# Where the first layer's Gelus stand beside a selective scan, and how its feature pipeline is paced

## The chip, the cores and the metric

The kernel runs on one core of one Trainium2 chip. The metric is the device time of one execution in microseconds; the median of three executions before the change is 9565.78 us (9564.62 to 9581.03). Five engines take part: TensorE (PE) for matmuls, VectorE (DVE), ScalarE (ACT), GpSimd (POOL) and SyncE (SP), whose queue issues the DMAs. Each engine works through its own instructions in order, and engines wait for one another by semaphores.

## The reference, cut to what matters

Four layers run one after another on an input of 4 images, 128 channels, 64x64 pixels. The change lies in layer 0, which is computed per image as follows (the names are those of the reference):

```python
feat = _gelu(_dwconv2d(x_adapted, conv1_w, conv1_b))           # first depthwise 3x3 convolution
ca = feat.mean((2, 3))
ca = sigmoid(maximum(ca @ ca1_w.T, 0.0) @ ca2_w.T)             # attention of channels
feat = _gelu(_dwconv2d(feat * ca[:, :, None, None], conv2_w, conv2_b))
scores = sigmoid(einsum('bchw,oc->bohw', feat, head_w)[:, 0] + head_b[0])
pv = jnp.var(x_adapted, axis=1, ddof=1)
final_scores = 0.7 * scores + 0.3 * sigmoid(pv * 10.0)
sm = final_scores.reshape(B, Hp, PS, Wp, PS).mean((2, 4)).reshape(B, Hp * Wp)
idx = jnp.argsort(-sm, axis=1)                                 # 256 patches of 4x4 pixels, sorted
...
x1n = layernorm(reordered x + pe[order])
...
dA = jnp.exp(dt[..., None] * A)
dBx = dt[..., None] * Bc[:, :, None, :] * xc[..., None]
def step(h, inp):                                              # selective scan over 4096 positions
    dA_t, dBx_t, C_t = inp
    h = dA_t * h + dBx_t
    return (h, jnp.einsum('bds,bs->bd', h, C_t))
...
out = (y * silu(z)) @ out_proj_w.T, put back in the old order
```

Before it stands a group norm of x (`_gn`). Layer 1 is a 3x3 convolution, layers 2 and 3 hold attention and expert layers; together they take the larger part of the time.

## The kernel before, in words

Layer 0 is the function `layers01`. For each of the four images (b = 0 to 3) there are two kinds of work.

The first kind is the generator `in_order(b, ...)`. It loads the image, computes the group norm (`K.groupnorm_scale`, L178), writes the normed image with a margin of one pixel (`xp`, by `K.groupnorm_fill`, L230 on ACT, eight chunks of 512 pixels), runs the first depthwise convolution with its Gelu (`first`), the attention of channels, the second convolution with its Gelu (`second`), the scores (`gauged`, with a Tanh), the sort of the patches (`sort`), the layer norm over positions (`ask`, `placed`, `centred`, `varied`, `scaled_by_root`), and at last the permutation (`turn`, `sorted_`), whose result `xq` is the sequence that the scan reads. The convolutions read their input in rows with 32 channels and three shifts laid over the partitions; so the padded image is stored to DRAM (`stored`, L458) and gathered again as `under` (`gather`, L467), three DMAs a chunk, all in SP's queue.

The second kind is `scan`. It goes through 32 chunks (4 images times 8 chunks of 512 positions). A chunk has eight groups g of two states each, and a group has two slots (i = 0 and 1), so that a chunk has 16 slots. A group begins on DVE with one multiplication (`hs`, L915) that reads `b_ps` from PSUM, where PE has spread the factors B (`spread_b`). Each slot then has two exponentials on ACT (`decay`, L922), two scans on DVE (L926), a copy of the last state (`carry`, L929) and a multiplication by C (L930) on POOL, and PE sums over states (`y_ps`, four matmuls in each odd slot, for the group before). There are two buffers for `decay` and one for `b_ps`.

The order of the scan stage is written out by hand: `tc.manual_schedule` keeps the order in which instructions are issued for all five engines. The order comes from turns. While the scan of image b runs, `in_order(b + 1)` is advanced by one turn in each slot, up to slot 110; what is left then is run at once in slot 111 (`until`, seven of eight chunks), since the entry of the next image's first chunk, in the eighth, reads `xq`. Two further things come beside the scans in each chunk: the entry of the next chunk (`enter`, with a Silu in slot 3, an Exp and a Ln in slot 7, POOL's work and eight DMAs `dt` and `dtx` in slots 8 to 11) and the gate (`gate`, issued in slot 8, its Silu in slot 9).

Matmuls are issued in the turn itself. What ACT, DVE or POOL does with their results is put off by `later` to the next `K.flush`, which comes in the next slot after that slot's two exponentials and before its scans. So a Gelu whose convolution is issued in an odd slot runs on ACT in the even slot that follows, behind that slot's exponentials. PE's part of a slot is issued in this order: `add` for the group before (odd slots), entry, turn, and in even slots `spread_b` at the end.

`staged(n, period, *stages)` is a software pipeline: every `period` turns another of n chunks starts, and each active chunk is advanced by one stage a turn. For both convolutions the stages are gather, nothing, nothing, convolution, nothing, next; `even()` waits for an even slot before each starts. `K.bank` gives out three PSUM banks in turn and flushes early where the oldest is still wanted. For b = 3 the scans have other work beside them (the end of images 2, 0 and 1), which is not touched.

For b = 0, `in_order` runs before the scans with nothing beside it, outside the hand-written order.

`Common` (L30 to L88) builds constants on DVE and POOL in one pool that stays for the whole kernel.

Of the kernel before, what the change touches and what calls it, by code (L numbers as in the profile page):

```python
# [30 lines left out]
class Common:  # L31
# [3 lines left out]
    def __init__(self, tc, pool):  # L35
# [33 lines left out]
        self.same4 = self.same_block("same4", 2)  # L69
        self.same16 = self.same_block("same16", 4)  # L70
        self.group_mean = pool.tile([P, P], F32, name="group_mean")
        nc.vector.tensor_scalar(self.group_mean, self.same4, 0.25, None, ALU.mult)

    def shifted(self, name, src, n, ops):

        nc = self.nc
        ti = self.pool.tile([P, n], I32, name=name + "_i")
        nc.vector.tensor_scalar(ti, src, *ops)
        tf = self.pool.tile([P, n], F32, name=name)
        nc.vector.tensor_copy(tf, ti)  # L80
        return tf

    def same_block(self, name, shift):
        nc = self.nc
        r = self.shifted(name + "_r", self.row_i, 1, (shift, None, ALU.arith_shift_right))
        c = self.shifted(name + "_c", self.col_i[:, 0:P], P, (shift, None, ALU.arith_shift_right))
        t = self.pool.tile([P, P], F32, name=name)
        nc.vector.tensor_scalar(t, c, r, None, ALU.is_equal)  # L88
        return t
# [194 lines left out]
def layers01(K, xd, dpool, w, w1):  # L284
# [8 lines left out]
    TURNS_END = 53  # L293
    ctx = ExitStack()
# [145 lines left out]
    def in_order(b, made, work, psum):  # L440
# [79 lines left out]
        yield from staged(NCH, 2, lambda c: gather(0, c), None, None, first, None, first_stored)  # L520
# [31 lines left out]

        def gauged(c):
# [5 lines left out]
            def tanh():  # L559
# [18 lines left out]
        for _ in range(2):  # L578
            next(tail)
            yield  # L580
# [3 lines left out]
        def sort():  # L584
            yield from wait(6)
# [49 lines left out]
        def centred(c):  # L635
# [42 lines left out]
        def scaled_by_root(n):  # L678
# [5 lines left out]
            def taken():  # L684
                rs = work.tile([P, CH], F32, name="ln_rs", tag="rs", bufs=1)
# [16 lines left out]
        yield from together(tail, sort(), staged(NCH, 2, ask, None, placed, centred, None, varied), backs())  # L702
# [1505 lines left out]
```

## Time and profile before

| | us |
|---|---|
| median of three executions | 9565.78 |
| the profiled execution | 9578.96 |
| its span, first to last instruction | 9577.2 |
| stage 1: `in_order(0)`, before the scans | 0 to 232 |
| stage 2: scans of images 0 to 2, `in_order(1 to 3)` beside them | 232 to 1976 |
| stage 3: scan of image 3, ends of images beside it | 1976 to 2638 |
| the rest: layers 1 to 3 | 2638 to 9577 |

The stages are told apart by the first multiplication L915 (232.4 us), by that of chunk 24 (1976.1 us) and by the last scan (2637.7 us). In the profile a line number is that of the kernel before. L92 is the matmul helper, and L144 is the line of `later`: instructions put off by it have its line, so they are told apart by the names of their tiles (`fp` is the first Gelu's output, `f` the second's, `sz` the gate's). A group of instructions is given with its number, busy time, mean duration of one, idle time of its engine before them and what ended that. "A <- B" in a list of waits means that A's engine stood idle and B's end released it.

### The profile page before, as it was taken

To read this page: it belongs to the slowest core of one execution; us is meant where nothing else is said; L and a number is where in the kernel's file an instruction comes from. 1 tells how busy PE (TensorE), PEld (TensorE's weight loads), DVE (VectorE), ACT (ScalarE), POOL (GpSimd) and SP (SyncE) were. 2 spreads that over 40 slices of the span, in tenths; PEclk is the share of its full clock that TensorE was granted. 3 is DMA by queue.
4 is the path that set the end of the run, shared out by engine and by line. 5 is a ranking of instruction groups with operands and counts; after the bars stand their busy time and mean duration, and the time that the engine had idled before them with its cause. 6 is when DMAs were issued, how large, how long until landed. Compare 5 with 4: busy or idle time off the path is not lost.

```text
span 9577.2 us, 189161 instructions
## 1 busy us (share of the span) xinstructions
PE 8608.8 (90%) x74394; PEld 3287.8 (34%) x74394; DVE 7159.3 (75%) x7845; ACT 7287.0 (76%) x10505; POOL 4933.0 (52%) x3287
## 2 busy tenths in 40 slices
PE   5887888889879999979999979999989999998787
PEld 2221222234443333333333333333333333334444
DVE  1889798987858888868888867888876888874464
ACT  3776767654449999969999969999978999984232
POOL 1677676765525555555555545555555555543011
PEclk8887888889989999989999989999989999999998
DMA  4434425222232221141222233221222222231205
GB/s 118 122 77 109 108 72 128 74 67 80 71 86 39 39 41 40 32 112 40 40 40 40 39 94 55 38 41 39 39 81 62 40 40 40 40 97 58 81 10 168
DMA packets 580323, 631.22 MB, mean 66 GB/s; under 512 B 118816, under 2 KB 374888, under 8 KB 578536
## 3 DMA queue, kind: packets, MB, share of 16 engines
q1 hardware_dynamic: 579432, 619.12, 27.5%
q8 instruction: 586, 9.60, 0.4%
q14 instruction: 305, 2.50, 0.1%
HBM read 444.74 MB, written 106.97 MB: 58 GB/s over the span
## 4 chain that ended last, share of the span: by engine, by line
PE 60%; DVE 4%; DMA 2%; POOL 2%; issue 2%; ACT 2%; SPq 0%; DVEq 0%; POOLq 0%; ACTq 0%
PE ctx_ps L92 27%; PE acc_ps L92 14%; PE score L92 12%; PE ln_xc L92 1%; DMA w<-in_L_ffn_weight 1%; PE hid_ps L92 1%; PE kv L92 1%; POOL ln_sd L1845 1%; PE ln_var L129 1%; DVE ctx L1498 0%; DMA queries<-head_d 0%; POOL q L1293 0%; PE pool L92 0%; DVE x L1998 0%; ACT hid L1685 0%
## 5 line engine op out<-in xcount | busy, mean ns | idle before, releaser
L1564 ACT ACTIVATE ex<-score 128x1024 f32<-128x1024 f32 x5120 | 4924.1, 1038 | 235.8 <-PE score L92 147.9
L92 PE MATMUL ctx_ps<-ex,qt 128*32 128x512 f32 x20480 | 2733.2, 606 | 19.7 <-DVE ctx L1498 19.7
L1513 POOL TENSOR_TENSOR folded<-ex 128x1024 f32<-128x1024 f32 x512 | 1223.3, 2389 | 2100.3 <-ACT ex L1564 1826.9
L1570 DVE STREAM_TRANSPOSE turned<-ex 128x1024 f32<-128x1024 f32 x1536 | 1885.3, 1227 | 337.1 <-ACT ex L1564 336.8
L1546 DVE STREAM_TRANSPOSE turned<-ex 128x1024 f32<-128x1024 f32 x1532 | 1841.9, 1202 | 0.0
L92 PE MATMUL acc_ps<-turned,turned_v 128*32 128x256 f32 x24576 | 1769.3, 379 | 3.0 <-POOL qt L1251 2.3
L926 DVE TENSOR_TENSOR_SCAN hs<-decay,carry,hs 128x512 f32<-128x512 f32 x1024 | 1245.4, 1265 | 196.9 <-ACT decay L922 183.8
L92 PE MATMUL score<-queries,keys 32*128 32x512 f32 x10240 | 1334.3, 497 | 51.9 <-POOL queries L1241 47.0
L92 PEld LDWEIGHTS acc_ps<-turned,turned_v 128*32 128x32 f32 x24576 | 800.8, 110 | 1476.6 <-issue 1324.4
L930 POOL TENSOR_TENSOR hs<-hs,c_sb 128x1024 f32<-128x1024 f32 x512 | 1207.0, 2357 | 70.4 <-DMA c_sb<-c_d 31.4
L922 ACT ACTIVATE decay<-dt,a_neg 128x512 f32<-128x512 f32 x1024 | 693.0, 689 | 659.8 <-DVE hs L926 649.8
L92 PEld LDWEIGHTS score<-queries,keys 32*128 32x128 f32 x10240 | 512.4, 182 | 1145.7 <-ACT ex L1564 777.7
L1370 POOL TENSOR_TENSOR turned_v<-v,quarter 128x1024 f32<-128x1024 f32 x256 | 612.9, 2395 | 264.8 <-PE acc_ps L92 222.5
L92 PE MATMUL y_ps<-hs,pair 128*64 128x512 f32 x2048 | 656.1, 769 | 32.2 <-POOL hs L930 32.2
L1514 POOL TENSOR_TENSOR quarters<-folded 128x512 f32<-128x512 f32 x512 | 657.6, 1284 | 40.1
L92 PEld LDWEIGHTS ctx_ps<-ex,qt 128*32 128x32 f32 x20480 | 406.4, 108 | 655.2 <-issue 599.1
L915 DVE TENSOR_TENSOR hs<-dtx,b_ps 128x2048 f32<-128x2048 f32 x256 | 579.8, 2265 | 54.9 <-PE b_ps L92 31.0
L92 PE MATMUL b_ps<-dbc,state 32*64 32x512 f32 x1024 | 340.8, 747 | 237.4 <-DVE hs L915 237.3
L929 POOL COPY carry<-hs 128x2 f32<-128x2 f32 x512 | 97.9, 191 | 688.3 <-DVE hs L926 659.6
L1564 ACT ACTIVATION_READ_ACCUMULATOR ex<-score 128x1 f32 x2048 | 439.0, 214 | 0.0
L1498 DVE COPY ctx<-ctx_ps 128x512 f32<-128x512 f32 x256 | 176.8, 691 | 329.3 <-PE ctx_ps L92 317.8
L1555 DVE TENSOR_REDUCE dacc<-quarters 128x2 f32<-128x512 f32 x508 | 326.9, 643 | 0.0
(376 smaller groups left out, 8785.0 us busy)
## 6 DMA issues: line engine op xcount, KB each, us to landing
c_sb<-c_d SPq DMA_DIRECT2D x512, 128.0 KB
keys<-head_d SPq DMA_DIRECT2D x1024, 64.0 KB
queries<-head_d SPq DMA_DIRECT2D x1024, 64.0 KB
under<-image_d SPq DMA_DIRECT2D x192, 264.0 KB
dt<-dt SPq DMA_DIRECT2D x128, 256.0 KB
dtx<-dtx SPq DMA_DIRECT2D x128, 256.0 KB
v<-value_d SPq DMA_DIRECT2D x1024, 32.0 KB
w<-in_L_ffn_weight SPq DMA_DIRECT2D x32, 1024.0 KB
```

The lines of the kernel that those rows point to most:

```text
L92: self.nc.tensor.matmul(out, lhsT, rhs, start=start, stop=stop)
L915: nc.vector.tensor_tensor(hs, dtx2, bb.unsqueeze(1).to_broadcast([P, NQ, CH]), ALU.mult)
L922: nc.scalar.activation(ex, dt2[:, q, :], AF.Exp, scale=a_neg[:, q, g : g + 1])
L926: nc.vector.tensor_tensor_scan(hs[:, q, :], decays[q - 2 * i], hs[:, q, :], carry[:, g, q : q + 1], ALU.mult, ALU.add)
L930: nc.gpsimd.tensor_tensor(hs[:, two, :], hs[:, two, :], cs.unsqueeze(1).to_broadcast([P, 2, CH]), ALU.mult)
L1370: nc.gpsimd.tensor_tensor(t, v.unsqueeze(2).to_broadcast([P, 4 * BT, 4, HD]), quarter.unsqueeze(1).to_broadcast([P, 4 * BT, 4, HD]), ALU.mult,
L1513: nc.gpsimd.tensor_tensor(hs, exs[:, :, 0], exs[:, :, 1], ALU.add)
L1514: nc.gpsimd.tensor_tensor(qs, hs[:, :, 0 : CH // 2], hs[:, :, CH // 2 :], ALU.add)
L1546: nc.vector.transpose(*upright)
L1555: nc.vector.tensor_reduce(at, qs, AX.X, ALU.add)
L1564: nc.scalar.activation(ex, sps[p], AF.Exp, scale=scale, accum_out=sums[:, t : t + 1] if summed else None)
L1570: nc.vector.transpose(*upright)
```

## The change

- In `staged` a new argument `quiet` names a stage. While any active chunk is about to run that stage, the whole pipeline is held until the slot within the chunk is one of 0, 8, 10, 12, 14 (`QUIET`). It is used for both convolutions of images 1 to 3 (stage 3 is the convolution; its Gelu follows in the next slot). For b = 0 it is off.
- The square for the patch variance (`pv_mean`, `pv_sq`) leaves `second` and becomes a stage of its own, `gauge`, one turn before the second convolution; `gauged` comes one turn later than before.
- For images 1 to 3 the padded image is filled two chunks in a turn.
- `sort` starts when all eight gauges are counted, instead of after a fixed number of turns; the two extra turns before it are gone.
- The position pipeline starts a chunk every 1.5 turns for images 1 to 3, instead of every 2.
- Tiles tagged `ln_sq` and `rs` get two buffers instead of one. To make room, the temporary tiles of `Common` move to a pool that is closed after use.

```diff
@@ -58,33 +58,35 @@
 
         self.row_i = pool.tile([P, 1], I32, name="row_i")
         nc.gpsimd.iota(self.row_i, pattern=[[0, 1]], base=0, channel_multiplier=1)
-        self.col_i = pool.tile([P, 256], I32, name="col_i")
-        nc.gpsimd.iota(self.col_i, pattern=[[1, 256]], base=0, channel_multiplier=0)
         self.col = pool.tile([P, 256], F32, name="col")
-        nc.vector.tensor_copy(self.col, self.col_i)
         self.row = pool.tile([P, 2], F32, name="row")
         nc.vector.tensor_copy(self.row[:, 0:1], self.row_i)
         nc.vector.tensor_scalar(self.row[:, 1:2], self.row[:, 0:1], 128.0, None, ALU.add)
 
-        self.same4 = self.same_block("same4", 2)
-        self.same16 = self.same_block("same16", 4)
-        self.group_mean = pool.tile([P, P], F32, name="group_mean")
-        nc.vector.tensor_scalar(self.group_mean, self.same4, 0.25, None, ALU.mult)
-
-    def shifted(self, name, src, n, ops):
+        with tc.tile_pool(reuse_waits="tile", name="temporary", bufs=1) as tmp:
+            self.col_i = tmp.tile([P, 256], I32, name="col_i")
+            nc.gpsimd.iota(self.col_i, pattern=[[1, 256]], base=0, channel_multiplier=0)
+            nc.vector.tensor_copy(self.col, self.col_i)
+            self.same4 = self.same_block("same4", 2, tmp, tmp)
+            self.same16 = self.same_block("same16", 4, tmp, pool)
...
@@ -291,6 +293,7 @@
 
     SLOTS = 2 * NG
     TURNS_END = 53
+    QUIET = (0, 8, 10, 12, 14)
     ctx = ExitStack()
     pool = lambda name, bufs, **kw: ctx.enter_context(tc.tile_pool(reuse_waits="tile", name=name, bufs=bufs, **kw))
     cst = pool("l0_const", 1)
@@ -402,11 +405,13 @@
             nc.sync.dma_start(out=t[:, at], in_=src[:, at])
         return t
 
-    def staged(n, period, *stages):
+    def staged(n, period, *stages, quiet=None):
 
 
         active, begun, turn = [], 0, 0
         while begun < n or active:
+            while any(a[1] == quiet for a in active) and K.slot % SLOTS not in QUIET:
+                yield
             if begun < n and turn >= begun * period:
                 active.append([begun, 0])
                 begun += 1
@@ -503,7 +508,9 @@
             fill(c)
             if c in (3, 5, 7):
                 stored(xp, 0, c // 2 - 1)
-            yield
+            if c % 2 or b == 0:
+                yield
+        quiet = 3 if b else None
         fp = kept["fp"] = big.tile([P, HW + 2, HW + 2], F32, name="fp", tag="mid")
         nc.gpsimd.memset(fp[:, 0, :], 0.0)
         nc.gpsimd.memset(fp[:, HW + 1, :], 0.0)
@@ -517,7 +524,7 @@
                 stored(fp, 1, c // 2)
 
         yield from even()
-        yield from staged(NCH, 2, lambda c: gather(0, c), None, None, first, None, first_stored)
+        yield from staged(NCH, 2, lambda c: gather(0, c), None, None, first, None, first_stored, quiet=quiet)
 
         def attention_of_channels():
             favg = small.tile([P, 1], F32, name="favg")
@@ -537,17 +544,16 @@
 
         begun = [0]
 
-        def gather_second(c):
-            gather(1, c)
-            begun[0] += 1
-
-        def second(c):
+        def gauge(c):
             mp = K.bank(psum, [P, CH], "pv_mean")
             mm(rect(mp), K.center, xp[:, 1 + 8 * c : 9 + 8 * c, 1 : HW + 1])
-            sq = squares[c] = work.tile([P, CH], F32, name="pv_sq", tag="ln_sq", bufs=1)
+            sq = squares[c] = work.tile([P, CH], F32, name="pv_sq", tag="ln_sq", bufs=2)
             later(nc.scalar.activation, sq, mp, AF.Square)
+
+        def second(c):
+            begun[0] += 1
             ps = convolved(unders.pop(c), deep2)
-            f2 = features[c] = work.tile([P, CH], F32, name="f2", tag="rs", bufs=1)
+            f2 = features[c] = work.tile([P, CH], F32, name="f2", tag="rs", bufs=2)
             later(nc.scalar.activation, f2, ps, AF.Gelu, bias=conv2_b, scale=ca)
 
         def gauged(c):
@@ -565,24 +571,29 @@
                     AX.XY,
                     ALU.add,
                 )
+                later(counted)
+
+            def counted():
+                gauges[0] += 1
 
             later(tanh)
 
-        seconds = staged(NCH, 2, gather_second, None, None, second, None, gauged)
+        gauges = [0]
+        seconds = staged(
+            NCH, 2, lambda c: gather(1, c), None, gauge, second, None, None, gauged, quiet=quiet
+        )
         channels = attention_of_channels()
         yield from even()
         tail = together(channels, seconds)
         while begun[0] < NCH:
             next(tail)
             yield
-        for _ in range(2):
-            next(tail)
-            yield
 
         perm = []
 
         def sort():
-            yield from wait(6)
+            while gauges[0] < NCH:
+                yield
             sp = K.bank(psum, [P, 256], "sm_ps")
             mm(sp, share.to_broadcast([P, P]), sm)
             later(nc.vector.tensor_copy, sm, sp)
@@ -639,7 +650,7 @@
             def taken():
                 if c == 0:
                     kept["xn"] = big.tile([P, 16, 256], F32, name="xn", tag="mid")
-                sq = squares[c] = work.tile([P, CH], F32, name="pos_sq", tag="ln_sq", bufs=1)
+                sq = squares[c] = work.tile([P, CH], F32, name="pos_sq", tag="ln_sq", bufs=2)
                 nc.scalar.activation(sq, mp, AF.Square)
                 for a in range(2):
                     nc.scalar.copy(inner(c, a), outer(mp, a))
@@ -682,7 +693,7 @@
                 nc.tensor.transpose(by_block[:, k], spreads[:, n, k : k + 1].to_broadcast([P, P]), K.ident)
 
             def taken():
-                rs = work.tile([P, CH], F32, name="ln_rs", tag="rs", bufs=1)
+                rs = work.tile([P, CH], F32, name="ln_rs", tag="rs", bufs=2)
                 nc.scalar.copy(rs, bp)
                 later(scaled, rs)
 
@@ -699,7 +710,7 @@
                 scaled_by_root(n)
                 yield from wait(2 if n < 4 else 1)
 
-        yield from together(tail, sort(), staged(NCH, 2, ask, None, placed, centred, None, varied), backs())
+        yield from together(tail, sort(), staged(NCH, 1.5 if b else 2, ask, None, placed, centred, None, varied), backs())
         yield
 
 
```

More of the change, by code (lines that the diff above doesn't have):

```diff
@@ L67, in __init__, with shifted, same_block @@
         nc.vector.tensor_scalar(self.row[:, 1:2], self.row[:, 0:1], 128.0, None, ALU.add)
-        self.same4 = self.same_block("same4", 2)
-        self.same16 = self.same_block("same16", 4)
-        self.group_mean = pool.tile([P, P], F32, name="group_mean")
-        nc.vector.tensor_scalar(self.group_mean, self.same4, 0.25, None, ALU.mult)
-    def shifted(self, name, src, n, ops):
+        with tc.tile_pool(reuse_waits="tile", name="temporary", bufs=1) as tmp:
[4 more added lines that the diff above has]
+            self.same16 = self.same_block("same16", 4, tmp, pool)
+            self.group_mean = pool.tile([P, P], F32, name="group_mean")
+            nc.vector.tensor_scalar(self.group_mean, self.same4, 0.25, None, ALU.mult)
+    def shifted(self, name, src, n, ops, pool=None):
         nc = self.nc
-        ti = self.pool.tile([P, n], I32, name=name + "_i")
+        pool = pool or self.pool
+        ti = pool.tile([P, n], I32, name=name + "_i")
         nc.vector.tensor_scalar(ti, src, *ops)
-        tf = self.pool.tile([P, n], F32, name=name)
+        tf = pool.tile([P, n], F32, name=name)
         nc.vector.tensor_copy(tf, ti)
         return tf
-    def same_block(self, name, shift):
+    def same_block(self, name, shift, tmp, pool):
         nc = self.nc
-        r = self.shifted(name + "_r", self.row_i, 1, (shift, None, ALU.arith_shift_right))
-        c = self.shifted(name + "_c", self.col_i[:, 0:P], P, (shift, None, ALU.arith_shift_right))
-        t = self.pool.tile([P, P], F32, name=name)
+        r = self.shifted(name + "_r", self.row_i, 1, (shift, None, ALU.arith_shift_right), tmp)
+        c = self.shifted(name + "_c", self.col_i[:, 0:P], P, (shift, None, ALU.arith_shift_right), tmp)
+        t = pool.tile([P, P], F32, name=name)
         nc.vector.tensor_scalar(t, c, r, None, ALU.is_equal)
```

## The prediction

> **What bounds the kernel now.** I began with the stages, because the change touches only the first two.
>
> ```profile
> core 0: us, PE busy (x) PEld busy (x) DVE busy (x) ACT busy (x) POOL busy (x), PEclk, DMA share, GB/s
> 0.00:232.00 232.00, 130.39 (x682) 50.41 (x682) 37.29 (x106) 77.48 (x115) 31.91 (x44) 0.89 0.45 111
> 232.00:1976.00 1744.00, 1428.29 (x5022) 420.85 (x5022) 1530.08 (x1230) 1194.80 (x1594) 1258.28 (x960) 0.83 0.39 98
> ```
>
> From 232 to 1976 us DVE is busy 1530 of 1744 us, more than any other engine. Its work there is fixed; what can be won is its idle time of 214 us. The waits of that stretch, and of three chunks of the first scan, say where it lies:
>
> ```profile
> DVE hs L926 <- ACT decay L922: 165.1, 97, 5.5
> ...
> DVE hs L926 <- ACT decay L922: 43.3, 21, 5.5
> ...
> DVE hs L926 <- ACT decay L922: 2.3, 3, 0.9
> ```
>
> The first line is the whole stage: 165 us of scans waiting for their exponentials. The second is chunks 1 to 3 of the first scan, where both convolutions run beside it; the same chunks of the next two show 44.1 and 42.5. The third is chunk 7, which has an entry and a gate but nothing else. So 130 of the 165 us come with the convolutions. The timeline of ACT and of DVE shows one such wait (slot 30):
>
> ```profile
> 355.31 1.28 ACT L144 ACT_TABLE_LOAD   x1
> 361.94 0.69 ACT L144 ACTIVATE fp<-conv,conv_b 128x512 f32<-128x512 f32 x1 [5.35 <-PE conv L92]
> 362.53 0.19 ACT L144 ACTIVATION_READ_ACCUMULATOR fp<-conv,conv_b 128x1 f32 x1
> 362.74 1.28 ACT L922 ACT_TABLE_LOAD   x1
> 364.03 1.30 ACT L922 ACTIVATE decay<-dt,a_neg 128x512 f32<-128x512 f32 x2
> ...
> 364.76 2.46 DVE L926 TENSOR_TENSOR_SCAN hs<-decay,carry,hs 128x512 f32<-128x512 f32 x2 [5.45 <-ACT decay L922]
> ```
>
> The Gelu sits between two table loads of 1.28 us, waits 5.35 us for its convolution, and the next exponentials stand behind it. The convolution was issued in the odd slot just before, and PE reached it late.
>
> **What each Gelu costs, before.** From the starts of the scans, with DVE's own work taken off, each slot's idle time follows. For the first eight Gelus (slots 28 to 42) it is 1.73, 5.41, 2.08, 0, 2.20, 3.97, 1.36 and 2.20 us, for the second eight with their Tanh (slots 48 to 62) 21.7 us together.
>
> **What one costs in an odd slot.** Behind an odd slot's scans (2.5 us) DVE has the multiplication L915 (2.26 us). How much of ACT's work this hides, other rows tell: the entry's Silus in slot 3 (1.28 + 0.69 + 0.68 + 1.28 = 3.93 us) leave 0.69 us of idle DVE; with a fill of 0.82 us in the same slot (4.75 us) 1.39 us. So about 3.3 us are free, and what exceeds them costs nearly all of itself. A Gelu with its two loads is 3.4 us (3.3 for `f`): 0.1 us.
>
> Here a rule speaks against the change. The Trainium skill ("ScalarE: Activation LUTs", What ACT_TABLE_LOAD costs) prices a switch of tables at 1283 ns and a drain of 1380 ns, 2.66 us in all. A Gelu would then take 6.2 us and cost 2.9 in each odd slot, and a gate slot with three switches 6.8; 36 and 12 of them make 186 us, more than the 130 lost now, so the kernel would come out some 75 us slower. The rows show the load alone: the exponential starts at 364.03, 1.29 us after its load began. I take 1.28.
>
> **The change, part by part**, for each of images 1 to 3:
>
> 1. *Gelus moved.* The order of the changed program puts the 16 Gelus in slots 25, 27, 29, 31, 33, 41, 43, 45 and 57, 59, 61, 63, 65, 73, 75, 77. Twelve are alone with their loads: 12 x 0.1 = 1.2 us. Four (25, 41, 57, 73) follow the gate's Silus in slot 9: 1.28 + 1.2 + 1.28 + 0.9 + 1.28 = 5.8 us, 2.4 us of DVE idle each, 9.6 in all. Entries in chunks 1 to 4 still wait some 1.2 us each, 5 us. The loads fall by only 12 in the whole program (446 to 434); they are not where the gain lies.
> 2. *Convolutions in even slots, PE.* The convolution (2.78 us) now stands ahead of `b_ps`, which the next L915 needs. In the trace PE stood idle 6.28 us before the `b_ps` at 340.22, waiting for L915 to release the bank, and that `b_ps` was done 3.3 us before it was needed: 6.28 - 2.78 + 3.3 = 6.8 us of slack. The Gelu no longer finds its convolution late. In turns of the second convolution PE's work for a group is 2.78 + 1.13 + 1.07 + 1.07 + 1.94 = 8.0 us against DVE's 4.80 + 2.26 + 0.66 = 7.7: seven groups, 2 us. If PE is cold (`b_ps` 1.97 us instead of 1.07), up to 7.
> 3. *SP's queue.* Gathers keep their three DMAs and three turns of lead; the first now stand ahead of the entry's `dt` and `dtx`, which wait for POOL. Behind a late gather stand the `c_sb` loads. Hidden, by the slack of part 2.
> 4. *Square apart, two buffers.* Square and Tanh (0.6 + 0.76 us) fall in even slots, under their 3.3 us: nothing; beside a Gelu they would cost 1.3 each.
> 5. *Fills in pairs.* 1.6 us of ACT in slots 14 to 17, under the same cover: nothing. It takes one fill out of slot 19, -0.7, which I leave in the rounding.
> 6. *What moves later.* Position work and sort go from chunks 4 and 5 (87.1 and 69.7 us in the trace) to 5 and 6, with eight positions in 12 slots instead of 16; the last `xq` falls in slot 111, a slot in which the rest runs in a burst. The instructions are the same, closer together, and POOL has 1.2 us more a position in the tight slots beside 2 x 2.55 a group. I take 4 us, and 1.5 for the burst (a permutation: transposes, copy, matmul, copy, about 5 us in the first stage, half of it hidden). Bounds -2 and +15.
>
> The second rule weighed bears on part 6. In the sort an operation of DVE that reads two SBUF tiles has these rows, beside the scans and in the first stage:
>
> ```profile
> L598 DVE SCALAR_TENSOR_TENSOR eq<-sm,cl,before x6: 2393/2412/2431, 561.8 to 1734.7; 128x256 f32<-128x256 f32 x6
> ...
> 143.85 0.48 DVE L598 SCALAR_TENSOR_TENSOR eq<-sm,cl,before 128x256 f32<-128x256 f32 x1
> ```
>
> 2.41 us instead of 0.48. The skill ("SBUF — State Buffer", SBUF: two separate sides) says why: such an operation and one of POOL take a shared pair of ports in turn, for a whole instruction. By the rule, with POOL fuller, all ten such operations of a sort could be held by some 2 us, 20 us in place of some 9 now (12.9 us in the trace's chunk 4, 3.9 by the shortest rows): +11 an image. By the rows most are held already, by the C multiplications that stay. I take 0 and keep +11 within the +15.
>
> Sum for an image: before 43.3 + 2.4 (chunk 4) = 45.7; after 1.2 + 9.6 + 5 + 2 = 17.8; gain 27.9, less 5.5 for part 6: 22.4. For three: 67.
>
> 7. *Stage 1.* Two things of it change the path:
>
> ```profile
> 19.62 2.39 SPq L402 DMA_DIRECT2D xb<-in_x  x4
> ...
> 46.84 8.72 PE L92 MATMUL conv<-under,deep 96*32 96x512 f32 x48 [13.82 <-DMA under<-image_d]
> ...
> 164.39 0.58 ACT L686 COPY ln_rs<-pos_rs 128x512 f32<-128x512 f32 x1 [1.76 <-POOL xn L691]
> ```
>
> With the temporary pool the weights' loads wait for DVE's constants, and the changed order puts the image ahead of them. The image lands by some 11 us (it took 9.8 in the trace), the constants by 13, the norm and fill by 24; the weights, 19 us of issuing, by 32. The stores of `xp` stand behind them: 32 instead of 35.3, without the fill's pace (4.5 us for four); convolutions near 41.5: -5.3, between 0 and -10. The second `rs` buffer frees ACT and POOL from one another in the five last scalings: 2.35 us becomes POOL's 1.7, -3.3. Together -8.
>
> Total -75. The profiled execution, 9578.96 us, would become 9504; it stands 13.2 us above the median, so for the median 9565.78 - 75 = 9491 us.
>
> **Rivals.** *A, as summed*: 9460 to 9520 alone. *B, the delayed position work gives much back*: part 6 costs 18 us an image instead of 5.5, as its full +15 and PE half cold would make it; (27.9 - 18) x 3 + 8 = 38, 9528 us. For it: chunk 4 already has PE waiting for POOL (41.5 us over the three scans, longest 6.8). Against: POOL is busy 62.8 of 87.1 us there. *C, a convolution holds up `b_ps`, slower*: if a gather lands late, PE stops in an even slot with `b_ps` behind, and L915 waits, DVE with it. The trace has convolutions waiting for `under` 17.4 us in 7 cases, 3.3 at most in the one before slot 30. It decides from the slack of 6.8 us: 75/48 = 1.6 us beyond it at each of 48 convolutions undo the gain, 2.8 us make it 9625. *D, no real change*: the holds only move the idle time, as ACT's 165 us partly turn into waits for PE; within 19 us of the time before.
>
> **How the numbers follow.** A 0.66, B 0.18, C 0.09, D 0.07. I call 0.2% (19 us) what a measurement can tell: A and B are faster (0.84), D the same (0.07), C slower (0.09). The range takes in A, B and the bounds of parts 6 and 7: from 9455 (part 6 at -2 in each image, -22; stage 1 at -13, -5; Gelus behind the gate at 1.7 us, -8) to 9545 (B, with nothing won in stage 1, and 9 us of chance).
>
> **What would show it.** Right: scans' waits for `decay` near 75 us over the stage instead of 165; none for Gelus in odd slots but some 2.4 us in slot 9; chunks 3 and 4 near 68 us, chunk 5 near 91; first convolution before 43 us. Wrong: a new row of L915 waiting for `b_ps` beyond today's 11.5 us (C), chunks 5 and 6 together over 170 us (B), a Gelu in an odd slot that costs over 1 us, or turns left in slot 111 that stop the scans for over 10 us.

## The result, and the profile after

The changed kernel takes 9513.76 us, the median of four executions (9509.44 to 9520.02); the kernel before, run beside it, takes 9565.2 us (four executions, 9560.02 to 9581.03). The ratio is 0.9938, with a 95% interval of 0.9925 to 0.9951: faster by 0.6%, beyond the 0.2% that the prediction took as the least that a measurement can tell. The forecast was 9491 (9455 to 9545), a gain of 75 us; 51 came.

The stages of the two profiled executions are told apart as before: the first multiplication of the scans, that of chunk 24, the last scan.

| us | before | after | difference | forecast |
|---|---|---|---|---|
| stage 1, before the scans | 232.4 | 218.6 | -13.8 | -8 |
| stage 2, scans of images 0 to 2 | 1743.7 | 1706.5 | -37.2 | -67 |
| stage 3, scan of image 3 | 661.6 | 657.9 | -3.7 | 0 |
| the rest, layers 1 to 3 | 6939.5 | 6928.7 | -10.8 | 0 |

In the rest the two programs have the same working instructions; over the profiled executions listed below it varies between 6913 and 6947 us, so its -10.8 need not come from the change. Stage 3's -3.7 lies in its fourth chunk (91.7 us before, 87.5 after), which takes 91.6 and 92.0 us in e1 and e8 below, so it need not either. Stages 1 and 2 give -51.0 together; the medians differ by 51.4.

In the profile after, the lines of the code are shifted: the multiplication L915 is now L926, the scans are L937, the exponentials L933, POOL's multiplication by C L941, the matmul helper L94, the helper of put-off instructions L146. First the two stages in the view of stretches (busy time of each engine, number of instructions in brackets):

```profile
core 0: us, PE busy (x) PEld busy (x) DVE busy (x) ACT busy (x) POOL busy (x), PEclk, DMA share, GB/s
0.00:218.60 218.60, 125.73 (x682) 49.92 (x682) 35.86 (x106) 77.22 (x115) 31.53 (x44) 0.86 0.48 118
218.60:1925.00 1706.40, 1419.20 (x5022) 421.36 (x5022) 1525.31 (x1230) 1180.31 (x1582) 1253.34 (x960) 0.83 0.40 101
```

DVE is busy as long as before (1525 us against 1530); its idle time fell from 214 to 181 us, not to the 147 that the forecast of -67 means. DVE's waits in stage 2, in the list of waits of the kernel after (total, number, longest), say why:

```profile
DVE hs L937 <- ACT decay L933: 73.6, 69, 2.7
DVE hs L926 <- issue: 32.6, 5, 7.1
DVE hs L926 <- PE b_ps L94: 28.1, 18, 2.8
...
DVE perm_s L731 <- PE perm_t L727: 11.1, 4, 4.8
DVE hs L926 <- POOL hs L941: 5.7, 1, 5.7
```

(The part left out before `perm_s` holds the wait of the very first multiplication, which belongs to stage 1, and the waits of `ln_vt`, 13.0 us against 13.3 before.) The waits of the scans for their exponentials fell from 165.1 to 73.6 us, where the forecast had "near 75". But the multiplication L926 has two rows that were not there: 32.6 + 5.7 = 38.3 us in six stops, two in each image, behind the scans of slots 31 and 63. "issue" and POOL are only what the profile puts the last semaphore down to. What the multiplication lacks is `b_ps`, as the timelines of the changed kernel around slot 31 show (start, duration, engine; in brackets the idle time before it and who ended it); first SP's queue:

```profile
331.88 3.03 SPq L829 DMA_DIRECT2D dt<-dt  x4
334.96 1.82 SPq L895 DMA_DIRECT2D c_sb<-c_d  x2
336.95 3.11 SPq L829 DMA_DIRECT2D dtx<-dtx  x4
340.16 1.97 SPq L472 DMA_DIRECT2D under<-image_d  x3
```

and PE and DVE:

```profile
348.45 5.35 PE L94 MATMUL conv<-under,deep 96*32 96x512 f32 x24 [6.66 <-DMA under<-image_d]
353.73 1.97 PE L94 MATMUL b_ps<-dbc,state 32*64 32x512 f32 x4
...
355.80 2.29 DVE L926 TENSOR_TENSOR hs<-dtx,b_ps 128x2048 f32<-128x2048 f32 x1 [7.14 <-issue]
```

The gather of the fourth convolution stands behind the four `dtx` loads, is issued at 340.16 to 342.13 us, and lands only by 348.45. PE waits 6.66 us for it, then takes 5.35 us for a convolution that takes 2.78 elsewhere, and `b_ps` stands behind: the prediction's rival C, in two of sixteen convolutions of an image.

A Gelu in an odd slot looks as foreseen. This is slot 29 on ACT:

```profile
332.43 1.28 ACT L146 ACT_TABLE_LOAD   x1
333.73 0.69 ACT L146 ACTIVATE fp<-conv,conv_b 128x512 f32<-128x512 f32 x1
334.31 0.19 ACT L146 ACTIVATION_READ_ACCUMULATOR fp<-conv,conv_b 128x1 f32 x1
334.52 1.28 ACT L933 ACT_TABLE_LOAD   x1
335.82 1.30 ACT L933 ACTIVATE decay<-dt,a_neg 128x512 f32<-128x512 f32 x2
```

It waits for nothing, each function starts 0.02 us after its load, and the next exponentials come 3.4 us after the first load; DVE's scans then wait 0.33 us; behind the gate in slot 25 they wait 2.73 us. In both, 0.11 us is a gap that stands there without a Gelu too.

```profile
329.23 4.81 DVE L937 TENSOR_TENSOR_SCAN hs<-decay,carry,hs 128x512 f32<-128x512 f32 x4 [2.73 <-ACT decay L933]
...
336.54 4.81 DVE L937 TENSOR_TENSOR_SCAN hs<-decay,carry,hs 128x512 f32<-128x512 f32 x4 [0.33 <-ACT decay L933]
```

### The profile page after: what moved, and what is told of

The parts are those of the page before. It is cut to its first block, busy times and chain, and to the rows that moved or that the text cites. A ratio compares the mean times of both kernels' runs of the same rounds, so it can differ in the third digit from the quotient of the medians.

```text
span 9511.7 us, 189086 instructions
## 1 busy us (share of the span) xinstructions
PE 8601.4 (90%) x74394; PEld 3291.5 (35%) x74394; DVE 7152.9 (75%) x7845; ACT 7275.5 (76%) x10493; POOL 4928.9 (52%) x3287
## 4 chain that ended last, share of the span: by engine, by line
PE 60%; DVE 4%; POOL 2%; issue 2%; ACT 2%; DMA 2%; SPq 1%; DVEq 0%; POOLq 0%; ACTq 0%
PE ctx_ps L94 28%; PE acc_ps L94 14%; PE score L94 12%; PE ln_xc L94 1%; PE hid_ps L94 1%; DMA w<-in_L_ffn_weight 1%; PE kv L94 1%; PE ln_var L131 1%; POOL ln_sd L1856 1%; DVE ctx L1509 0%; SPq L1244 0%; PE pool L94 0%; DVE x L2009 0%; POOL q L1304 0%; ACT hid L1696 0%
## 5 line engine op out<-in xcount | busy, mean ns | idle before, releaser
L94 PE MATMUL ctx_ps<-ex,qt 128*32 128x512 f32 x20480 | 2734.0, 606 | 19.8 <-DVE ctx L1509 19.8
L94 PE MATMUL acc_ps<-turned,turned_v 128*32 128x256 f32 x24576 | 1769.3, 379 | 3.0 <-POOL qt L1262 2.3
L94 PE MATMUL score<-queries,keys 32*128 32x512 f32 x10240 | 1333.7, 497 | 39.1 <-POOL queries L1252 33.4
L937 DVE TENSOR_TENSOR_SCAN hs<-decay,carry,hs 128x512 f32<-128x512 f32 x1024 | 1242.6, 1265 | 104.7 <-ACT decay L933 92.6
L94 PEld LDWEIGHTS acc_ps<-turned,turned_v 128*32 128x32 f32 x24576 | 800.5, 110 | 1476.9 <-issue 1324.3
L941 POOL TENSOR_TENSOR hs<-hs,c_sb 128x1024 f32<-128x1024 f32 x512 | 1207.4, 2358 | 80.8 <-DMA c_sb<-c_d 40.8
L933 ACT ACTIVATE decay<-dt,a_neg 128x512 f32<-128x512 f32 x1024 | 692.7, 689 | 646.5 <-DVE hs L937 637.5
L94 PEld LDWEIGHTS score<-queries,keys 32*128 32x128 f32 x10240 | 512.4, 182 | 1133.3 <-ACT ex L1575 775.5
L94 PE MATMUL y_ps<-hs,pair 128*64 128x512 f32 x2048 | 642.7, 754 | 35.6 <-POOL hs L941 35.3
L926 DVE TENSOR_TENSOR hs<-dtx,b_ps 128x2048 f32<-128x2048 f32 x256 | 580.7, 2268 | 110.5 <-PE b_ps L94 47.7
L94 PEld LDWEIGHTS ctx_ps<-ex,qt 128*32 128x32 f32 x20480 | 406.1, 108 | 655.5 <-issue 599.4
L94 PE MATMUL b_ps<-dbc,state 32*64 32x512 f32 x1024 | 328.3, 722 | 181.3 <-DVE hs L926 181.1
```

The costliest lines, as they stand in the source:

```text
L94: self.nc.tensor.matmul(out, lhsT, rhs, start=start, stop=stop)
L926: nc.vector.tensor_tensor(hs, dtx2, bb.unsqueeze(1).to_broadcast([P, NQ, CH]), ALU.mult)
L933: nc.scalar.activation(ex, dt2[:, q, :], AF.Exp, scale=a_neg[:, q, g : g + 1])
L937: nc.vector.tensor_tensor_scan(hs[:, q, :], decays[q - 2 * i], hs[:, q, :], carry[:, g, q : q + 1], ALU.mult, ALU.add)
L941: nc.gpsimd.tensor_tensor(hs[:, two, :], hs[:, two, :], cs.unsqueeze(1).to_broadcast([P, 2, CH]), ALU.mult)
```

## Experiments

Each was profiled and timed beside the kernel before. "Stage 2" is from its profiled execution, after 1706.5 and 1743.7 us for the changed kernel and the one before.

| run | us, median | ratio to before, 95% | stage 2 |
|---|---|---|---|
| e1_no_hold | 9577.85 | 0.9993 to 1.0012 | 1781.2 |
| e2_dtx_later | 9572.33 | 0.9986 to 1.0005 | 1770.9 |
| e3_spread_first | 9544.7 | 0.9951 to 0.9975 | 1722.9 |
| e4_odd_conv | 9550.77 | 0.9955 to 0.9981 | 1751.0 |
| e5_after_again | 9511.04 | 0.9923 to 0.9947 | 1703.2 |
| e6_gather_early | 9488.58 | 0.9896 to 0.9926 | 1688.7 |
| e7_stage1_only | 9545.71 | 0.9961 to 0.9982 | 1735.4 |
| e8_small_dtx | 9483.18 | 0.9885 to 0.9920 | 1686.4 |
| e9_early_small | 9459.11 | 0.9862 to 0.9892 | 1667.5 |
| e10_four_in_a_row | 9497.95 | 0.9903 to 0.9933 | 1699.2 |
| e11_early_again | 9487.99 | 0.9890 to 0.9923 | 1681.9 |

The theory at the start: the hold does what was forecast to the exponentials, and what is missing of the gain is the late convolution with `b_ps` behind it. The rivals: that the rest of the change, not the hold, brings the gain; that the order of `b_ps` is to blame; that SP's order is; that the bandwidth of the DMA engines is.

**Without the hold.**

```diff
-        quiet = 3 if b else None
+        quiet = None
```

> The changed kernel without the hold (the pipelines of both convolutions run freely, so that Gelus fall in even slots again, beside entry and gate); all its other parts stay. Theory (the hold carries the gain beside the scans): scans wait for decay some 150 us again over the stage of the three scans, that stage is back near 1740 us, and only the first stage's 14 us are kept: 9540 to 9556 us. Rival (the other parts, buffers, pairs and period 1.5, carry it): 9525 us or less.

9577.85 us: no faster than the kernel before, and outside what both expected. Stage 1 keeps its gain (217.3 us), and stage 2 is 37 us slower than before. The list of waits of this kernel:

```profile
DVE hs L937 <- ACT decay L933: 144.4, 83, 5.7
DVE perm_s L731 <- PE perm_t L727: 41.4, 12, 5.5
DVE sm L146 <- ACT two_t L566: 27.6, 12, 4.1
```

Chunks 2 to 5 take 81 to 88 us each. The waits for `perm_s` and `two_t`, of the permutation and of the second convolution's scores, are 69 us here and 12 in the changed kernel (6.6 before the change). So the hold is worth 1781 - 1706 = 75 us beside the rest of the change, more than the whole gain, and the denser order without the hold costs; that was not foreseen. The hold with the old, looser order was not tried, so what it is worth by itself stays open.

**`dtx` two slots later**, to let the gather pass it.

```diff
             later(twice, dt2, dt)
             yield
+            yield
+            yield
             later(nc.gpsimd.tensor_tensor, dtx, dt, xc, ALU.mult)
```

> The changed kernel with the entry's last product and its four dtx loads issued two slots later, so that the fourth chunk's gather comes ahead of them and the fifth's behind them. Theory (a gather that lands behind the dtx transfers is late, its convolution stops PE, and b_ps and the group's first multiplication wait behind it): the two long waits of an image leave slots 31 and 63 and turn up one group later, in slots 33 and 65, where DVE has 1.5 us more to do; six waits of 4 to 7 us, total 9500 to 9515 us. Rival (PE's own load or a buffer of hs makes these waits): they stay in slots 31 and 63, within 3 us of the changed kernel.

The two stops moved to slots 33 and 65 and shrank (4.0 and 3.3 us in the first image), as the theory said, but the time, 9572.33 us, missed its 9500 to 9515:

```profile
DVE hs L928 <- DMA dtx<-dtx: 97.2, 24, 16.6
DVE hs L939 <- ACT decay L935: 68.5, 64, 2.7
DVE hs L928 <- PE b_ps L94: 51.9, 27, 4.3
```

The longest, 16.6 us, is the first multiplication of all, at the start of the scans, as in the changed kernel. Beside it, the first multiplication of nearly every chunk waits 1.5 to 5.6 us for its `dtx`. `dtx` has no two slots to give; the gather has to come before it.

**`b_ps` ahead of the convolution.**

```diff
                     due = math.inf if K.slot + 1 >= until else pace * (K.slot + 1 - begin)
                     turns = 0
+                    if i == 0 and (g + 1 < NG or more):
+                        bb = spread_b(*divmod(m, NG))
...
-                    if i == 0 and (g + 1 < NG or more):
-                        bb = spread_b(*divmod(m, NG))
```

> The changed kernel with b_ps issued on PE ahead of the turn's convolution in each even slot, instead of behind it. Theory (a late convolution holds b_ps up): the six long waits of the group's first multiplication (38 us) go, but each convolution now starts only when that multiplication of the group before has freed the bank, and Gelus come late: scans wait for decay some 30 to 70 us more; 9505 to 9550 us. Rival (the long waits come from something else, a buffer or POOL): they stay, and so does the time, within 5 us.

9544.7 us, within what the theory gave. The multiplication's long waits are gone, and the scans' wait for `decay` is 115.5 us instead of 73.6: the late convolution now holds its Gelu, and the Gelu the exponentials. Putting `b_ps` first only moves where the late gather is paid. Stage 2 lost 16 us by it; another 16 came in stage 3 (673.9 us instead of 657.9), which the edit reaches too and where these convolutions do not run.

**Convolutions in odd slots.**

```diff
-    QUIET = (0, 8, 10, 12, 14)
+    QUIET = (1, 9, 11, 13, 15)
```

> The changed kernel with the hold set to slots 1, 9, 11, 13, 15: convolutions in odd slots, Gelus in the even slots behind them, none beside a gate's Silu. Theory (what matters is that the convolution is done when its Gelu's turn comes, and that L915's multiplication covers the Gelu): the 2.6 us beside each gate go (31 us), the long waits go, but every Gelu finds its convolution late by 1 to 2 us, as in the kernel before: 9520 to 9545 us. Rival (it is enough to keep Gelus away from entry and gate): 9500 us or less.

9550.77 us, beyond the 9520 to 9545 of the theory and far from the rival's 9500. The stops are gone, and the Gelus no longer stand beside the gate's Silu. But stage 2 is 1751 us and the waits for `decay` are 143.2 instead of 73.6: the first Gelu of each row (slots 26, 42, 58 and 74) costs 2.2 us and some later ones 3 to 7, though a few cost only 0.1 (slot 28); in an odd slot one costs at most 0.2. That the Gelus keep away from entry and gate is not enough; the fall of these waits needs the parity. A wait of the sort's `sm` of 31 us came in addition (1.2 in the changed kernel); its cause stays open.

**Stage 1's part alone**: the kernel before with the temporary pool of `Common` as in the change, and with the second buffers for `pv_sq`, `pos_sq`, `f2` and `ln_rs`, of which one line stands here.

```diff
-            sq = squares[c] = work.tile([P, CH], F32, name="pv_sq", tag="ln_sq", bufs=1)
+            sq = squares[c] = work.tile([P, CH], F32, name="pv_sq", tag="ln_sq", bufs=2)
...
```

> The kernel before with the temporary pool for the constants and the second buffer for the tags ln_sq and rs, and none of the rest (no hold, no square apart, no pairs of fills, period 2). Theory: stage 1 gains what it gained in the changed kernel, 12 to 16 us, and the stage beside the scans stays within 8 us of 1744; 9550 to 9556. Rival: the second buffers let POOL and ACT run ahead beside the scans and change those too, by more than 10 us in either direction.

Stage 1 is 218.9 us, as in the changed kernel, so these parts are enough for its -13.8, though the changed kernel gets there in part by another road (see below). Stage 2 is 8.3 us shorter than before, just beyond the 8 that the theory allowed; its waits for `decay` are 143.8 us instead of 165.1. The medians differ by 29 us (9574.72 before, 9545.71), almost half of what the changed kernel gains against the same runs (9511.04, below). That second buffers help beside the scans too was booked at nothing.

**The gathers one turn earlier**, with the changed kernel again beside it.

```diff
-        quiet = 3 if b else None
+        quiet = 4 if b else None
+        lead = (None,) * (3 if b else 2)
...
-        yield from staged(NCH, 2, lambda c: gather(0, c), None, None, first, None, first_stored, quiet=quiet)
+        yield from staged(NCH, 2, lambda c: gather(0, c), *lead, first, None, first_stored, quiet=quiet)
...
-            NCH, 2, lambda c: gather(1, c), None, gauge, second, None, None, gauged, quiet=quiet
+            NCH, 2, lambda c: gather(1, c), *lead[1:], gauge, second, None, None, gauged, quiet=quiet
```

> The changed kernel itself, as the measure for the other two runs on the same chip: 9513 us, within 10 us, and again two idle stretches of the multiplication of 6 to 7 us in each image, in slots 31 and 63.

> The changed kernel with every gather of the held convolutions one turn earlier (one stage more between gather and convolution, the hold one stage later), so that on SP's queue the gathers of the fourth convolution stand ahead of the four dtx loads of slot 27 and of slot 59 instead of behind them; nothing else moves. Theory (the order on SP's queue puts the gather behind dtx, whose product is late, and the convolution then holds b_ps): the two idle stretches of the multiplication in slots 31 and 63, 38 us over three images, go; since each gather now waits for the convolution before last to release its buffer, dtx may come up to 2 us later, and some of the first multiplications of chunks 2 and 4 may wait 1 to 2 us. Time: 25 to 40 us below the changed kernel, 9475 to 9490. Rival (bandwidth: the 1 MB of dtx and the gathers together are too much for the time, in whatever order): the wait moves to the first multiplication of chunks 2 and 4, behind dtx, and the time stays within 10 us of the changed kernel.

The control gave 9511.04 us, with six stops of 35.6 us in all. The early gathers gave 9488.58, 22 us less, and 9487.99 in another run (below): faster than both kernels, though short of the 25 to 40 expected. The list of waits of the kernel with early gathers:

```profile
DVE hs L938 <- ACT decay L934: 72.4, 66, 2.7
DVE hs L927 <- PE b_ps L94: 45.8, 25, 6.1
```

The rows of the stops are gone, and the waits for `b_ps` rose by 17.7 us. In slot 63 nothing is left. In the first convolution the stop moved from the fourth Gelu (slot 31) to the fifth (slot 33: the multiplication waits 6.1, 3.4 and 3.6 us in the three images), whose gather now stands behind `dtx`. In the other run of this kernel only the first image has it (6.0 us), the others 2.4 and 2.9 us in slot 31, and the waits for `b_ps` are 40.4 us: this stop varies from one execution to another. Neither theory was right alone: roughly half of the stops was SP's order. The other half needed its own test.

**`dtx` in its place in the queue, but 16 KB instead of 1 MB**, in the changed kernel and in the one with early gathers.

```diff
-            dt2, dtx2 = (work.tile([P, NQ, CH], F32, name=name) for name in ("dt2", "dtx2"))
+            dt2 = work.tile([P, NQ, CH], F32, name="dt2")
+            dtx2 = work.tile([P, NQ, 8], F32, name="dtx2")
...
-            later(twice, dtx2, dtx)
+            later(twice, dtx2, dtx[:, :, 0:8])
...
-                nc.vector.tensor_tensor(hs, dtx2, bb.unsqueeze(1).to_broadcast([P, NQ, CH]), ALU.mult)
+                nc.vector.tensor_tensor(hs, dt2, bb.unsqueeze(1).to_broadcast([P, NQ, CH]), ALU.mult)
```

> The changed kernel with the four dtx loads of each entry left in their place on SP's queue, still waiting for POOL's product, but carrying 8 of 512 columns (16 KB instead of 1 MB); the multiplication takes dt in place of dtx, so dtx and what follows from it are left out of the computation. Theory (the stalls of slots 31 and 63 are mostly bandwidth: dt, dtx, the gathers and the image's stores together keep all 16 DMA engines full from 333 to 353 us): the gather behind dtx lands some 3 us after its issue instead of 6 to 8, and the long waits of the multiplication fall from 38 us over three images to under 12. Rival (order alone: SP reaches the gather too late, since dtx waits for POOL): the gather is issued as late as before, and over 25 us of the 38 stay.

> The kernel with the early gathers, with the same small dtx loads; dtx and what follows from it are left out of the computation. In the kernel with early gathers the wait of slot 31 became one of slots 33 and 35 (7.2 and 3.1 us in the first image, 3 to 7 us in the others): the fifth gather, issued at 342.4 to 344.5 us, landed by 353. Theory (bandwidth): both go, chunk 2 falls from 69 to 75 us to 66 to 68, and the stage beside the scans comes to 1650 to 1672 us. Rival (the wait is due to something else in SP's order, such as the store of fp ahead of the gather): chunk 2 stays over 69 us.

In the list of waits of the changed kernel with small `dtx`, the stops are 15.0 + 3.8 = 18.8 us instead of 38.3, between the two theories:

```profile
DVE hs L927 <- issue: 15.0, 5, 4.9
...
DVE hs L927 <- POOL hs L942: 3.8, 2, 3.4
```

The gather behind `dtx`, and its convolution:

```profile
338.91 1.50 SPq L472 DMA_DIRECT2D under<-image_d  x3
...
344.92 5.31 PE L94 MATMUL conv<-under,deep 96*32 96x512 f32 x24 [3.73 <-DMA under<-image_d]
```

It lands 4.5 us after the last of its three issues (340.41 to 344.92) instead of 6.3 (342.13 to 348.45). The theory had 3 us for this and under 12 us of stops. Counted from the entry's first `dt` load, the gather's issue ended 1.0 us earlier and the gather landed 2.8 us earlier, so 1.8 us are a faster landing. So the bytes of `dtx` account for about half of the stops, and the place in the queue for the other half. With both removed, early gathers and small `dtx`, the stops shrink to 4.2 us in two: chunk 2 takes 65.1, 64.8 and 65.3 us, below the 66 to 68 expected, and stage 2 1667.5 us. The stages add up in the same way: 1703 and 1706 us with neither, 1682 and 1689 with early gathers, 1686 with small `dtx`, 1668 with both. In the first image PE still waits for the gather of the fifth convolution, but the convolution runs at full speed and DVE does not notice:

```profile
349.88 2.78 PE L94 MATMUL conv<-under,deep 96*32 96x512 f32 x24 [1.97 <-DMA under<-image_d]
352.59 1.07 PE L94 MATMUL b_ps<-dbc,state 32*64 32x512 f32 x4
```

The view of stretches of 5 us shows how full the transfers are. The changed kernel:

```profile
323.00:328.00 5.00, 3.33 (x16) 0.79 (x20) 3.50 (x3) 4.94 (x7) 4.92 (x4) 0.52 0.00 0
...
333.00:338.00 5.00, 5.00 (x26) 0.98 (x26) 4.67 (x4) 4.22 (x7) 4.92 (x4) 0.61 0.99 227
338.00:343.00 5.00, 3.79 (x24) 0.69 (x16) 5.00 (x4) 4.47 (x6) 4.41 (x5) 1.00 1.06 228
343.00:348.00 5.00, 0.00 (x0) 0.00 (x0) 4.67 (x5) 3.75 (x6) 2.04 (x2) 0.91 1.07 218
348.00:353.00 5.00, 4.55 (x24) 1.13 (x24) 0.66 (x1) 0.34 (x1) 3.55 (x3) 0.50 1.06 283
```

and with the small `dtx`:

```profile
338.00:343.00 5.00, 3.19 (x16) 0.68 (x12) 4.80 (x4) 4.63 (x6) 4.54 (x5) 1.00 0.66 143
```

The columns at the end are PE's granted clock, the share of the 16 DMA engines and GB/s. Between 333 and 353 us the changed kernel moves some 4.8 MB (the four rates, 5 us each) with a share of 1 throughout, after a stretch without any traffic, in which SP's queue stands before the `dt` loads. A gather is 0.79 MB (3 x 264 KB), `dt` and `dtx` 1 MB each. The share alone proves nothing, for with early gathers and small `dtx` it is near 1 there too: loads that need not wait move up. What counts is whose bytes are ahead.

**Four convolutions in a row instead of five**, on top of the early gathers.

```diff
+    BUSY = (2 * SLOTS,)
...
-            while any(a[1] == quiet for a in active) and K.slot % SLOTS not in QUIET:
+            while any(a[1] == quiet for a in active) and (K.slot % SLOTS not in QUIET or K.slot in BUSY):
```

> The kernel with the early gathers, without the convolution in slot 32 (the fifth in a row of the first eight): its gather is asked for as before and gets five more slots to land, the other three of the first eight follow two slots later each, in slots 42 to 46, and the second eight stay where they are. Theory (five gathers beside dt and dtx are more than the DMA engines carry in that stretch, four are not): the waits of slots 33 and 35 go, chunk 2 falls from 69 to 75 us to 65 to 68, the stage beside the scans comes to 1668 to 1678 us; 10 to 20 us below the kernel with the early gathers alone. Rival: dt and dtx of the next chunk in slots 40 to 43 meet the gathers and stores of the last four, and the wait comes back in slots 43 to 47; within 5 us of the kernel with the early gathers alone.

> The kernel with the early gathers again, as the measure for the run beside it on the same chip: a ratio to the kernel before of 0.990 to 0.992, with the waits in slots 33 and 35.

Chunk 2 took 65.0, 68.0 and 68.1 us, inside the 65 to 68 of the theory, and the wait of slot 33 went. But in the run beside it chunk 2 took 74.5, 66.3 and 66.6, so only the first image gained. The time did not fall: 9497.95 against 9487.99, a difference within the 0.2% taken as the least that can be told; stage 2 of the profiled executions is 17 us longer. The trace shows what ate the gain, and neither theory named it. The eighth Gelu of the first convolution comes two slots later, and with it the attention of channels, whose Sigmoid and two loads now run in slot 53 together with six other instructions, most of them the entry's: the scans behind it wait 6.1, 6.1 and 6.6 us, and the waits for `decay` are 89.0 us instead of 75.4:

```profile
446.38 4.81 DVE L939 TENSOR_TENSOR_SCAN hs<-decay,carry,hs 128x512 f32<-128x512 f32 x4 [6.12 <-ACT decay L935]
```

Of the kernels that compute the whole, early gathers with five in a row were not beaten: 0.9906 of the time before in the last run, 0.9911 in the one before.

## Why the prediction was right, and where its sum failed

The direction, the range (9455 to 9545) and the mechanism of the gain hold; the size does not, by 23 us: 51 came of 75.

- *Part 1, the Gelus.* Right. The forecast took 30 us an image off the waits for `decay`, 90 in all; 165.1 - 73.6 = 91.5 were measured; with the second buffers and no hold, 143.8 and 144.4 us of these waits stay (e7 and e1), so some 70 of the 91.5 need the hold. A Gelu alone costs 0.0 or 0.22 us for 0.1, one behind the gate 2.62 for 2.4 (the gap of 0.11 us taken off). The second kind adds 12 x 2.62 = 31 us of what is left.
- *The price of a table switch.* The prediction took the row (the load alone, 1.28 us) against the Trainium skill ("ScalarE: Activation LUTs", What ACT_TABLE_LOAD costs), which adds a drain of 1380 ns and by the prediction's own working would have made the change slower by 75 us. The row decides here: the slots of the hold leave no place for a drain.
- *Parts 2 and 3, the failed step.* "6.28 - 2.78 + 3.3 = 6.8 us of slack" for the convolution ahead of `b_ps`, and for the gathers "Hidden, by the slack of part 2". Both terms failed. The slack was read in the old order, where PE is free 11.6 us before the multiplication wants `b_ps` (333.94 to 345.52 us). In the new one it is free 6.9 us before: PE is free at 341.79 us (348.45 - 6.66) and the multiplication wanted `b_ps` at 348.66 (355.80 - 7.14); a convolution of 2.78 and a `b_ps` of 1.07 leave 3.0 us. And the lateness was not priced: 6.66 us for the gather, 2.57 for the convolution at the lower clock (5.35 instead of 2.78) and 0.90 for `b_ps` (1.97 instead of 1.07), 10.1 us, of which 10.1 - 3.0 = 7.1 stop DVE. Six such stops are 38.3 us. The prediction saw that the gathers pass the entry's loads, but looked only at those that come first; the fourth comes behind them. And it did not add up the bytes that the hold brings together. The `b_ps` of 1.97 us from which it read its slack was itself one that came after 6.28 us of waiting; it took that slower clock as a bound only. The two rows of the kernel before:

```profile
340.22 1.97 PE L92 MATMUL b_ps<-dbc,state 32*64 32x512 f32 x4 [6.28 <-DVE hs L915]
...
345.52 2.26 DVE L915 TENSOR_TENSOR hs<-dtx,b_ps 128x2048 f32<-128x2048 f32 x1
```

- *The rest of stage 2.* Without the stops it would be 1706.5 - 38.3 = 1668 us; the run with small `dtx` and early gathers, which has 4.2 us of them left, has 1667.5. That is -76, better than the forecast -67, and the terms behind it are not those of the forecast. The forecast charged 6 us for PE and 16.5 for part 6; measured were about 12 to 17 more of waits for `b_ps` (12.4 in the control, 16.6 in the trace after) and 10 more for `perm_s`, less 5 us of DVE's own work and 5 of waits for `two_t`. Chunks 5 and 6 together took 158 us, not over 170: rival B did not come. The waits before, with which those of the list after are compared:

```profile
DVE hs L915 <- PE b_ps L92: 11.5, 11, 2.8
DVE sm L144 <- ACT two_t L560: 5.8, 3, 1.9
...
DVE perm_s L720 <- PE perm_t L716: 0.8, 3, 0.3
```

- *The sort.* The prediction left its `eq` rows unchanged and kept +11 us an image in the range, for the rule on shared ports. Beside the scans `eq` still takes 2.42 us, and chunk 5 is 86.3 us where 91 were forecast: the +11 did not come.
- *Part 7, stage 1.* Right in kind, too small: -13.8 for -8. The first convolution starts at 39.5 us (forecast 41.5): -7.4, of which 5.7 are left at its end. In the five last scalings the copies now wait 1.02 us instead of 1.76; from the fourth copy to the eighth they take 6.5 us instead of 9.4, 2.9 for the forecast 3.3:

```profile
39.48 7.25 PE L94 MATMUL conv<-under,deep 96*32 96x512 f32 x48 [23.32 <-DMA under<-image_d]
...
156.92 0.59 ACT L697 COPY ln_rs<-pos_rs 128x512 f32<-128x512 f32 x1 [1.02 <-POOL xn L702]
```

The rest came in the second convolution of stage 1, for which the prediction's part 7 has no term: its last chunks follow one another every 4.8 us instead of 5.8, and it ends 11.2 us earlier. The second buffers alone did not do that, for e7 has them and keeps 5.7 us; what e7 lacks there is the square as a stage of its own and the later `gauged`, which were not tried one by one. So e7 comes to nearly the same time by another road: its second convolution starts 2.6 us earlier than the changed kernel's and ends 2.9 us later.
- *Rival C* was given 0.09, and was priced for all 48 convolutions coming late. It came at 6 of them, and took 38 us, half of the forecast gain instead of all. The sign that the prediction named for it, waits for `b_ps` beyond 11.5 us, came too: 28.1 us beside the stops.

## What to carry to other kernels

When a change packs a step into fewer slots, add up what its transfers and those of everything else in these slots move, and follow the last of the packed steps through the DMA queue, not the first: here the fourth gather stood behind a 2 MB entry. Slack in front of a shared engine belongs to an order of work; read it again with the moved work in place, and with that engine at its slow clock if it has just waited. A late transfer has two remedies, an earlier place in the queue and fewer bytes ahead of it, and half a loss may belong to each.

## What the runs showed of the hardware

PE came back from 6.66 us of waiting at half speed: 24 matmuls of the convolution took 5.35 us, with a granted clock of 0.50 in that stretch, against 2.78 us at 1.00 where it had waited 1.97. In the five traces compared (before, after, e6, e8, e9) every convolution of stage 2 behind a wait of 3.1 us or more took 4.4 to 5.4 us, and every one behind a wait of 1.0 to 1.5 us at full clock took 2.78. Between 1.7 and 3.0 us both occur. These rows are from the changed kernel and from the one with early gathers:

```profile
398.28 5.35 PE L94 MATMUL conv<-under,deep 96*32 96x512 f32 x24 [2.29 <-ACT sz L146]
...
493.52 2.78 PE L94 MATMUL conv<-under,deep 96*32 96x512 f32 x24 [2.96 <-DMA under<-image_d]
```

The Trainium skill ("TensorE: Matmul & The Clock Gate", The HAM clock gate) gives just this halving after an idle window of some 3.4 us, and says that the windows run freely. The halving agrees; the length of a single wait does not decide it here, since 2.29 us were enough in one place and 2.96 not in another. So a late load in front of PE cost up to 2.6 us more than the wait, which the prediction had only as a bound.

A load landed later the more bytes had been issued ahead of it in its queue: a gather landed 6.3 us after its issue behind 1 MB of `dtx`, with all 16 DMA engines at a share of 1 and 218 to 283 GB/s, and 4.5 us after its issue behind 16 KB.
